# Who copies turned weights, z and values out of their banks: ScalarE by name instead of the tracer's choice, in an attention, feed-forward and state-space kernel

## The chip, the cores and the metric

The kernel runs on one core of one Trainium2 chip. The core has five engines, each with an instruction queue that it works off in order: TensorE (PE; its weight loads are listed apart as PEld), VectorE (DVE), ScalarE (ACT), GpSimd (POOL) and SyncE (SP, which here only issues DMAs). TensorE writes its results into eight banks of 128 x 512 fp32 each, the PSUM; they have to be copied or computed out of there by VectorE or ScalarE into the on-chip memory, the SBUF, before TensorE can take them as an operand again. The metric is device time in microseconds, the median of several executions.

## What is computed

Two sequences of 1024 rows of 256 numbers go through four residual layers, each on a layer norm of what came before:

```
x = x + attention(layernorm(x))            # 16 heads of 128, causal, ALiBi bias
x = x + ternary_ffn(layernorm(x))          # silu(gate) * up, rms norm, ternary weights
x = x + state_space(layernorm(x))          # in_proj, conv, scan over time, out_proj
x = x + kept_two_ffn(layernorm(x))         # silu(gate) * up, the 2 largest of 4 kept
```

The change lies in the attention, for which the reference is, cut:

```
q, k, v = x @ Wq.T, x @ Wk.T, x @ Wv.T                     # per head: (1024, 128)
scores = clip(q @ k.T / sqrt(128), -1024, 1024) + alibi_and_causal_mask
attn = softmax(scores)
out = sum over heads of (attn @ v) @ Wo_head.T
```

## The kernel before

The work is cut into four chunks k of 512 rows: sequence b = 0 or 1 and half u = 0 or 1 of it (`CH`). For each chunk the 16 heads of the attention are worked off one after another (`attention`, L397), and each head in four tiles j of 128 queries. A chunk with u = 1 sees 1024 keys; it takes the first 512 of k and v back from DRAM, where the chunk with u = 0 stored them head by head.

A step of a head is one tile j. In it:

- `scores` (L370): q times k into a bank `s` (PE, L377), clipped into the SBUF tile `ss` (VectorE, L381), the bias added and the row extreme `nm` found (VectorE, L387), then Exp with the row sum (ScalarE, L392).
- `turn` (L289), two steps later: PE turns the 128 x 128 blocks of the weights `ss` into a bank `pt` (L296), up to four blocks to a bank, and the bank is copied into `pT` (L299). A tile needs one such copy when u = 0 and two when u = 1: 2 x 16 x 4 x (1 + 2) = 384 in all, of 128 x 128, 256, 384 or 512 elements.
- `values` (L301), three steps later and only after each second tile, so for 256 queries at a time: v times the turned weights into a bank `z` (L308), copied into `zs`, 128 x 256 (L314): 128 copies.
- `project` (L316), four steps later: `zs` times the output weights into a bank `o` (L323); VectorE scales it and adds it to x (L329).
- for the next head, at tiles 0, 1 and 3: `queries`, `keys` (PE L336, copied with a scale by ScalarE, L343 and L350) and `new_values` (PE L360 into a bank `pv`, copied into `v`, 128 x 512, L365): 64 copies. If u = 0, SyncE then stores `v` in DRAM (L368).

The banks `pt`, `z`, `o`, `pq`, `pk` and `pv` are all taken in turn from one set of three (`ps_mm`, `ps_z`, L75), so each of these matmuls waits until the bank used three allocations before has been emptied. Two banks are for `s`, one for `y` of the state-space layer and two (`ps_r`) for the other layers.

While the heads of chunk k run, the remaining three layers of chunk k - 1 are worked off between them (`rest`, L969): after each step the loop at L992 draws as much of the other layers as its costs (`cost`, L974) make due. The last chunk's three layers come after all heads. The state-space layer is a scan over time on VectorE (L779, `hs`) for each of 64 pairs of a channel group and a state; ScalarE makes its decay `da` (L772) in a bank of `ps_r`, GpSimd its input `db` (L758) and its weighted output `hc` (L793), DMAs bring the rows `bs` and `cs` (L713), and PE sums the outputs up in `y` (L723). The softplus steps `se`, `sv`, `dl`, `sr` (L577 to L594) come once for each channel group.

The program is recorded by a tracer that lays out each engine's queue and sets the semaphores. An instruction written as `nc.scalar...` or `nc.vector...` goes to that engine; one written as `nc.any...` is given by the tracer to VectorE or ScalarE, one instruction at a time. The order in a queue is not strictly that of the program text. Besides the three copies of the change, `nc.any` stands at L148 (24 copies), L665 and L678 (4 each).

## Time and profile before

| | us |
|---|---|
| median of 3 runs | 1859.64 (1858.1 to 1860.81) |
| the profiled execution | 1863.3 |
| its span, first to last instruction | 1861.4 |
| PE busy | 1735.5 |
| DVE busy | 1308.0 |
| ACT busy | 947.3 |
| POOL busy | 821.3 |

How the three kinds of copies are shared out, with busy times:

| copy | on ScalarE | on VectorE |
|---|---|---|
| `pT` (L299) | 247, 115.8 us | 137, 69.7 us |
| `zs` (L314) | 56, 20.6 us | 72, 30.1 us |
| `v` (L365) | 53, 30.8 us | 11, 7.5 us |

Stages, in us from the span's start, read off from where each line runs: 0 to 280, chunk 0's heads alone, beside the preparation of ternary weights; 280 to 352, 790 to 838 and 1200 to 1268, heads beside the ternary feed-forward layer's end and the state-space layer's projections; 352 to 600, 838 to 1012 and 1268 to 1500, heads beside the scans of chunks 0, 1 and 2; 600 to 790, 1012 to 1200 and 1500 to 1640, heads beside the feed-forward layers; from 1640 on, chunk 3's other layers without heads.

A row of the profile names the line, the engine, the operation, what is written and read (out<-in, by the program's names without buffer numbers) and the shape. "Idle before" is the time that the engine stood still just before such instructions, with what ended it. PEclk and "granted clock" are the share of full speed that TensorE's clock was given.

### The profile page before, as it was taken

What the parts mean: (1) busy time and instruction counts of PE and PEld (TensorE: products, weight loads), DVE (VectorE), ACT (ScalarE), POOL (GpSimd) and SP (SyncE); (2) the same over time, 40 slices, a digit from 0 to 9 for tenths busy, and PEclk for the clock granted to TensorE, in tenths of its full rate; (3) what the DMA queues carried; (4) which work ended last, traced back from release to release, by engine and by line L of the source; (5) the groups of instructions that cost most, each with busy time, mean ns of one, the idle gap of its engine ahead of it and who ended that gap; (6) DMA issues with size and microseconds to landing.
All of it is one profiled execution on the core that took longest, in us unless ns stands there. A gap on an engine that the chain in (4) does not pass through costs nothing.

```text
span 1861.4 us, 25366 instructions
## 1 busy us (share of the span) xinstructions
PE 1735.5 (93%) x8468; PEld 1249.4 (67%) x8468; DVE 1308.0 (70%) x2552; ACT 947.3 (51%) x1736; POOL 821.3 (44%) x674
## 2 busy tenths in 40 slices
PE   8999999989989999997777999998998899998899
PEld 5777776566666667755555667765666676775895
DVE  5887656588875574568888465557888755857975
ACT  3445474545543553755554464565455436535742
POOL 3333040498873000418998001308898600035970
PEclk9999999989999999998989999999999899999999
DMA  6444412466652313127778424126675521212531
GB/s 192 153 145 156 151 57 86 145 213 206 201 182 83 105 51 121 56 93 234 217 230 233 142 68 141 39 85 225 196 229 172 168 100 50 74 53 77 183 129 62
DMA packets 178306, 256.07 MB, mean 138 GB/s; under 512 B 16240, under 2 KB 90992, under 8 KB 177152
## 3 DMA queue, kind: packets, MB, share of 16 engines
q1 hardware_dynamic: 176752, 241.61, 41.1%
q0 software_dynamic: 1152, 12.58, 1.8%
q8 instruction: 67, 1.10, 0.2%
q14 instruction: 63, 0.52, 0.1%
q10 hardware_dynamic: 272, 0.26, 0.0%
HBM read 232.04 MB, written 22.35 MB: 137 GB/s over the span
## 4 chain that ended last, share of the span: by engine, by line
PE 63%; DVE 11%; POOL 10%; issue 6%; DMA 5%; ACT 4%; SPq 1%; POOLq 0%; DVEq 0%; ACTq 0%
PE s L377 9%; PE z L308 8%; PE pq L336 5%; POOL hc L793 5%; PE pk L336 5%; PE pt L296 4%; PE o L323 4%; DVE hs L779 4%; PE pv L360 4%; POOL db L758 3%; PE g_g L463 3%; PE in L630 3%; PE u_g L463 3%; DMA cs<-bcd 3%; PE y L723 2%
## 5 line engine op out<-in xcount | busy, mean ns | idle before, releaser
L793 POOL TENSOR_TENSOR hc<-hs,cs 128x512 f32<-128x512 f32 x256 | 343.4, 1360 | 30.9 <-PE y L723 20.4
L381 DVE SCALAR_TENSOR_TENSOR ss<-s,lower 128x512 f32<-128x512 f32 (+3 forms) x384 | 205.5, 550 | 185.2 <-PE s L377 183.9
L392 ACT ACTIVATE ss<-ss,nm 128x128 f32<-128x128 f32 (+7 forms) x256 | 198.6, 776 | 255.1 <-DVE nm L387 238.3
L377 PE MATMUL s<-kT,qT 128*128 128x512 f32 (+3 forms) x768 | 301.6, 496 | 2.0 <-DVE ss L381 2.0
L758 POOL TENSOR_TENSOR db<-du,bs 128x512 f32<-128x512 f32 x192 | 267.1, 1400 | 67.2 <-DVE hs L779 44.8
L308 PE MATMUL z<-pT,v 128*128 128x256 f32 (+1 forms) x1280 | 274.0, 360 | 3.2 <-ACT pT L299 3.0
L308 PEld LDWEIGHTS z<-pT,v 128*128 128x128 f32 x1280 | 238.6, 191 | 49.3 <-ACT pT L299 4.9
L387 DVE CUSTOM_DVE_ANT_0 ss<-ss,alibi 128x128 f32<-128x128 f32 (+7 forms) x256 | 256.9, 1003 | 5.4
L772 ACT ACTIVATE da<-dl,a_neg 128x512 f32<-128x512 f32 x256 | 178.1, 697 | 140.5 <-DVE hs L779 110.7
L377 PEld LDWEIGHTS s<-kT,qT 128*128 128x128 f32 x768 | 134.9, 195 | 95.3 <-issue 85.1
L299 ACT COPY pT<-pt 128x512 f32<-128x512 f32 (+3 forms) x247 | 115.8, 486 | 161.7 <-PE pt L296 160.7
L779 DVE TENSOR_TENSOR_SCAN hs<-da,carry,db 128x512 f32<-128x512 f32 x128 | 160.0, 1270 | 31.2 <-POOL hc L793 19.8
L723 PE MATMUL y<-ident,hc 128*128 128x128 f32 x1024 | 152.5, 284 | 23.6 <-POOL hc L793 23.5
L296 PE MATMUL pt<-ident,ss 128*128 128x128 f32 x1152 | 170.9, 275 | 2.7 <-DVE x L329 2.7
L779 DVE TENSOR_TENSOR_SCAN hs<-da,db 128x512 f32<-128x512 f32 x128 | 153.2, 1210 | 19.0 <-POOL hc L793 11.0
L336 PE MATMUL pq<-xT_a,wq 128*128 128x512 f32 x256 | 135.8, 654 | 31.9 <-DVE zs L314 25.5
L723 PEld LDWEIGHTS y<-ident,hc 128*128 128x128 f32 x1024 | 125.1, 147 | 52.3 <-POOL hc L793 31.5
L296 PEld LDWEIGHTS pt<-ident,ss 128*128 128x128 f32 x1152 | 139.9, 142 | 18.1 <-DVE x L329 3.1
L323 PE MATMUL o<-wo,zs 128*128 128x256 f32 x512 | 135.6, 385 | 13.3 <-DVE zs L314 10.5
L360 PEld LDWEIGHTS pv<-wv,xT_a 128*128 128x128 f32 x1024 | 125.1, 197 | 18.1 <-ACT pT L299 14.1
L360 PE MATMUL pv<-wv,xT_a 128*128 128x128 f32 x1024 | 131.0, 282 | 5.0 <-ACT pT L299 4.6
L336 PE MATMUL pk<-xT_a,wk 128*128 128x512 f32 x256 | 127.1, 620 | 7.9 <-ACT qT L343 4.0
(204 smaller groups left out, 2547.7 us busy)
## 6 DMA issues: line engine op xcount, KB each, us to landing
cs<-bcd SPq DMA_DIRECT2D x256, 256.0 KB, 3.8
bs<-bcd SPq DMA_DIRECT2D x192, 256.0 KB, 4.5
alibi<-alibi_d SPq DMA_DIRECT2D x32, 512.0 KB, 4.7
wq<-in_wqT_dram SPq DMA_DIRECT2D x64, 128.0 KB, 2.6
wk<-in_wkT_dram SPq DMA_DIRECT2D x64, 128.0 KB, 2.5
wv<-in_wvT_dram SPq DMA_DIRECT2D x64, 128.0 KB, 3.2
wo<-in_woT_dram SPq DMA_DIRECT2D x64, 128.0 KB, 3.0
alibi<-alibi_d SPq DMA_DIRECT2D x32, 256.0 KB, 3.4
```

What stands on the lines that cost most here:

```text
L296: nc.tensor.transpose(tp[:, i, :], s[:, (kb0 + i) * P : (kb0 + i + 1) * P], ident)
L308: nc.tensor.matmul(zp[:, q0:W], lhsT=st["v_all"][:, kb, :], rhs=st["pts"][kb // 4][:, kb % 4, at * P + q0 : at * P + W], start=(kb == 0), ...
L323: ended["by"] = nc.tensor.matmul(op[:, i, :], lhsT=st["z"][half][:, i * P : (i + 1) * P], rhs=st["o"], start=True, stop=True,)
L336: nc.tensor.matmul(pp, lhsT=st[n][:, c, :], rhs=xT[:, c, :], start=(c == 0), stop=(c == KC - 1))
L360: nc.tensor.matmul(vp[:, t, :], lhsT=xT[:, c, t * P : (t + 1) * P], rhs=st["v"][:, c, :], start=(c == 0), stop=(c == KC - 1),)
L377: nc.tensor.matmul(sp[:, :n], lhsT=st["qT"][:, j * P : (j + 1) * P], rhs=st["kT"][:, k0 : k0 + n], start=True, stop=True,)
L381: nc.vector.scalar_tensor_tensor(s[:, k0 : k0 + n], sp[:, :n], CLIP, lower[:, S - W + k0 : S - W + k0 + n], op0=ALU.min, op1=ALU.max,)
L387: pace["tile"] = nc.vector.tensor_tensor_reduce(out=s[:, :W], in0=s[:, :W], in1=st["alibi"][:, :W], scale=1.0, scalar=3.0e38, op0=ALU.add, ...
L723: nc.tensor.matmul(yTs[c][:, t * P : (t + 1) * P], lhsT=h[:, t * P : (t + 1) * P], rhs=ident, is_transpose=True, start=start and t == 0, s ...
L758: nc.gpsimd.tensor_tensor(db[i], du, brow.pop(i), ALU.mult)
L779: nc.vector.tensor_tensor_scan(out=hs[i], data0=da.pop(i), data1=db.pop(i), initial=0.0 if first else carry[:, n, c : c + 1], op0=ALU.mult ...
L793: nc.gpsimd.tensor_tensor(hc[i], hs.pop(i), crow.pop(i), ALU.mult)
```

## The change

Three lines: the copy of the turned weights, the copy of z and the copy of the new values out of their banks are written as ScalarE's copy instead of the engine-neutral one. What is copied, where to, and the place in the program text stay.

```diff
@@ turn
-            nc.any.tensor_copy(st["pts"][kb0 // 4][:, 0:n, j * P : (j + 1) * P], tp[:, 0:n, :])
+            nc.scalar.copy(st["pts"][kb0 // 4][:, 0:n, j * P : (j + 1) * P], tp[:, 0:n, :])
@@ values
-        nc.any.tensor_copy(st["z"][half], zp[:, :W])
+        nc.scalar.copy(st["z"][half], zp[:, :W])
@@ new_values
-        nc.any.tensor_copy(v, vp)
+        nc.scalar.copy(v, vp)
```

## The prediction, made before the changed kernel was run

> **What bounds the kernel now.** I read the page's engine rows first, then the table of stages, then PE's waits in the stages where PE has gaps, then the chain of waits, the copies' own rows, and last one stall in order of time. From the page (engine: busy time, share of the span, instructions; then the granted TensorE clock in 40 slices):

> ```profile
> PE 1735.5 (93%) x8468; PEld 1249.4 (67%) x8468; DVE 1308.0 (70%) x2552; ACT 947.3 (51%) x1736; POOL 821.3 (44%) x674
> ...
> PEclk9999999989999999998989999999999899999999
> ```

> TensorE is the main bound, VectorE has more to do than ScalarE, and the clock dips in a few slices. The table of stages tells where (stage in us, its length, then busy time of PE, PEld, DVE, ACT, POOL with instruction counts, the granted clock, the DMA share, GB/s):

> ```profile
> 352.00:600.00 248.00, 223.86 (x1127) 164.87 (x1126) 197.19 (x353) 120.41 (x216) 188.31 (x137) 0.94 0.59 187
> 600.00:790.00 190.00, 188.74 (x858) 134.80 (x857) 107.78 (x244) 102.53 (x166) 24.26 (x21) 1.00 0.25 82
> ...
> 838.00:1012.00 174.00, 132.96 (x689) 95.18 (x687) 145.96 (x213) 88.55 (x182) 161.65 (x126) 0.94 0.76 228
> ...
> 1268.00:1500.00 232.00, 208.34 (x1037) 152.63 (x1036) 189.42 (x338) 113.84 (x204) 188.34 (x137) 0.94 0.61 193
> ```

> From 600 to 790 (attention beside a feed-forward layer) TensorE has 1.3 us of gaps; copies have nothing to win there, and the other stages without scans look the same (10.9 us of gaps from 0 to 280, mostly the first layer norm; 4 us or less in each of the rest). After 1640 there are no attention copies. So the change matters in the three stages with scans, C (352 to 600), E (838 to 1012) and G (1268 to 1500): PE gaps of 24, 41 and 24 us, and a clock of 0.94, worth 0.06 x 248 = 15, 10 and 14 us more. What ends PE's gaps in C (who waits <- for whom: us in total, times, longest):

> ```profile
> PE pq L336 <- DVE zs L314: 13.0, 5, 4.3
> PE o L323 <- DVE zs L314: 4.6, 2, 2.4
> PE pq L336 <- ACT zs L314: 2.5, 1, 2.5
> PE pv L360 <- ACT pT L299: 2.4, 2, 2.2
> ```

> Of 24 us, 17.6 wait for VectorE's copy of z (the weighted values) out of its bank; pq needs that bank, one of three, and o needs the copy itself. G answers alike: 12.5 + 2.9 = 15.4 of 23.5 us. In E, zs on VectorE ends only 3.0 of 41 us and hc on GpSimd 22.2; there the chain goes through the DMAs of cs, GpSimd's products and bs, so E hardly moves.

> How one such stall arises, in order of time (start, length, engine, line, operation, [idle before, and what ended it]):

> ```profile
> 381.90 1.89 DVE L387 CUSTOM_DVE_ANT_0 ss<-ss,alibi 128x640 f32<-128x640 f32 x1
> 382.04 0.68 ACT L772 ACTIVATE da<-dl,a_neg 128x512 f32<-128x512 f32 x1
> ...
> 383.73 1.74 DVE L591 TENSOR_TENSOR sr<-se,sr 128x512 f32<-128x512 f32 x1
> 383.84 0.83 ACT L392 ACTIVATE ss<-ss,nm 128x640 f32<-128x640 f32 x1 [1.12 <-DVE nm L387]
> ...
> 385.39 2.32 DVE L779 TENSOR_TENSOR_SCAN hs<-da,db 128x512 f32<-128x512 f32 x2
> ...
> 387.68 0.41 DVE L314 COPY zs<-z 128x256 f32<-128x256 f32 x1
> ...
> 388.15 1.22 PE L336 MATMUL pq<-xT_a,wq 128*128 128x512 f32 x1 [4.33 <-DVE zs L314]
> ```

> The last z matmul ends at 381.7. Its copy takes 0.41 us but stands 5.9 us in VectorE's queue, behind a score reduction, a softplus step and two scans. ScalarE is idle meanwhile, from 382.7 to 383.8 and again for 1.87 us before 386.6, each time held by an instruction that itself waits for VectorE.

> **The change part by part.** Of 576 copies (384 pT, 128 zs, 64 v), 356 are ScalarE's already (247 + 56 + 53); for these only the writing changes. 220 change engine:

> ```profile
> L299 ACT COPY pT<-pt 128x512 f32<-128x512 f32 x142 | 81.2, 580 | 128.4 <-PE pt L296 127.5
> ...
> L299 DVE COPY pT<-pt 128x512 f32<-128x512 f32 x50 | 34.1, 681 | 2.2 <-PE pt L296 2.1
> L314 DVE COPY zs<-z 128x256 f32<-128x256 f32 x72 | 30.1, 418 | 24.9 <-PE z L308 24.7
> ```

> (count | busy us, mean ns | idle before.) VectorE loses 50 x 0.681 + 42 x 0.547 + 34 x 0.279 + 11 x 0.412 for pT, 72 x 0.418 for zs and 11 x 0.682 for v: 34.1 + 23.0 + 9.5 + 4.5 + 30.1 + 7.5 = 108.7 us, and goes from 1308 to about 1200. ScalarE gains the same shapes at its own rows (580, 473, 252, 373; 368; 580 ns): 29.0 + 19.9 + 8.6 + 4.1 + 26.5 + 6.4 = 94.5 us, from 947 to 1042, 56% of the span. Both totals lie beside TensorE's 1735 and are no time by themselves.

> Out of banks, then, ScalarE is 15% shorter on the same shape (580 against 681 ns). [...]

> In C the moves are 24 pT, 13 zs and 2 v (12.7 + 5.4 + 1.4 = 19.4 us off VectorE), in G 23, 11 and 2 (17.6 us), in E 6, 8 and 1 (6.1 us). C's ScalarE rises by some 17 us, from 120 to 137 of 248.

> *PE's stalls.* In C and G together the 24 zs on VectorE cost PE 17.6 + 15.4 = 33.0 us, the 8 on ScalarE 5.0 us: 0.63 each. The 81 pT on ScalarE (42 + 39) cost 2.9 + 4.4 = 7.3 us, 0.09 each; the 47 on VectorE nothing. If copies that move fare like those already there: zs 32 x 0.63 = 20 instead of 38, pT 47 x 0.09 = 4.2 more, net 13.8 us fewer stalls.

> *The clock.* After the 4.33 us stall the clock reads 0.50 from 388.1 to 391.9 and four pq take 3.78 us; after one of 2.44 us before 371.3 it reads 0.50 from 373 to 375; after one of 1.40, from 416 to 418, it reads 1.00. Over C and G 28.8 us of clock loss stand beside 47.4 us of gaps, 0.61 for each, so 13.8 us of stalls bring 8.4 more: 22 us of PE time at best. [...]

> *Not all of it reaches the end.* Cut to C and G, the chain of waits spends 157 us on PE, 138 on VectorE, 86 on GpSimd. VectorE's moved copies hold 8.0 us of it directly (zs 3.1 + 2.4, pT 1.2 + 1.4); ScalarE, with 9% of its time on the chain (22 of 234), gives back 0.09 x 32 = 3. So the least gain by this reading is 5 us, the most 22. I take 14, near the middle: PE and VectorE hold similar shares of this chain.

> *What waits behind a moved copy.* On ScalarE: da (which feeds the scans), Exp, qT and kT. Copies of 0.25 to 0.58 us are covered there: da's own idle time before it, held by scans that have not freed its bank, is 110.7 us in the whole run, and no scan waits for da among VectorE's larger waits. If that cover went, the most is the 32 us added in C and G. v's DMA on SyncE follows its copy; the stored values are read a whole chunk later, so this costs nothing, at worst 11 x 0.58 = 6 us if each were waited for.

> *Order.* The tracer lays out each queue anew, and neighbours may move as well. No row prices that; I bound it by the stalls at stake, 22 us either way, and take nothing.

> **The sum.** The profiled execution took 1863.3 us (span 1861.4), 3.7 above the median of 1859.6. 1863.3 - 14 = 1849.3, and on the median's footing 1845.6: **1846**.

> **The rivals.**
> - *Slower: the copies queue behind a waiting Exp.* ScalarE works strictly in order, and its longest wait is Exp for VectorE's nm: 238.3 us in all, 50.9 in C, 47.8 in G. Before 415.8 it stood 3.79 us so, just when VectorE's zs ended a PE stall of 1.40. A zs placed after such an Exp comes 0.99 + 0.19 us later (Exp's mean in C, and its read of the sum), although z was ready. The deciding point: 32 r + 4.2 = 38.0, so beyond r = 1.06 us of stall for each zs the stages get longer (the eight seen have 0.63). If all 24 moved ones pay 1.18 more, PE loses 28 + 4 us before the clock's share; if half do, 14 + 4. With some of it off the chain: +4 to +30, most likely 1874. For it: at 415.8 VectorE took zs just while ScalarE stood held. Against: ScalarE is half idle and freeing VectorE also brings nm earlier.
> - *Much faster.* All zs stalls of C and G go: 38 + 0.61 x 38 = 61 us of PE time, of which VectorE (178 of C's 248 left) and GpSimd (188) let half through: 30 to 45, so 1815 to 1830.
> - *No change in time.* The copies move, the stages stay held by GpSimd's products and the DMAs of bs and cs, as E is now: 1856 to 1863. Should the written engine do less than it says (the 356 already there), it ends here too.

> **How the numbers follow.** Forecast (gain 5 to 22, so 1838 to 1855) 0.47; much faster 0.10; no change 0.13; slower 0.30. About 0.2% (3.7 us) is what a measurement of this kernel can tell from no change. Faster 0.57, same 0.13, slower 0.30. The range reaches into both outer cases, 1822 to 1877, and leaves out some 0.06 below and 0.12 above.

> **What would show it.** Right: all 576 copies as ACT; DVE near 1200 and ACT near 1042; PE's waits for zs in C and G down from 38 to about 20; clock there 0.95 or more; C and G each about 7 us shorter; all else in place. Wrong: "PE <- ACT zs" or "PE <- ACT pT" of 30 us or more, with ScalarE held by nm just before; or stalls gone and C and G as long, ended by hc, db or bs.

## The result: 1880.0 us, slower by 1.15%

The changed kernel takes 1880.01 us (median of 4 runs, 1878.54 to 1885.05) where the kernel before takes 1859.66: a ratio of 1.0115 with a 95% interval of 1.0095 to 1.0135. The forecast was 1846 in a range of 1822 to 1877; the time lies above both. For the copies of z the mechanism is that of the rival "the copies queue behind a waiting Exp", which had 0.30 and a price of 1874; the sign that the prediction named for it came, PE waiting 56.4 us for zs on ScalarE. More than half of the loss, though, comes only when the turned weights are forced to ScalarE too, and how it does was not isolated.

The profiled execution took 1880.1 us, its span is 1878.3, 16.9 more than before. From its page (engine: busy us, share, instructions; then the granted clock):

```profile
PE 1735.7 (92%) x8468; PEld 1248.4 (66%) x8468; DVE 1218.1 (65%) x2331; ACT 1018.0 (54%) x1957; POOL 820.3 (44%) x674
...
PEclk9999999999999999998998999999999999999999
```

PE's work is the same to 0.2 us. The copies moved as announced: 221 instructions fewer on VectorE and 221 more on ScalarE, VectorE relieved by 90 us. Yet the span grew. Where, tells the table of stages of the kernel after, cut at the same points of the work (stage, length, busy PE, PEld, DVE, ACT, POOL with counts, clock, DMA share, GB/s): first chunk 0's heads, then C, E and G.

```profile
20.30:224.00 203.70, 202.76 (x1031) 145.68 (x1030) 144.52 (x395) 106.71 (x285) 58.28 (x51) 1.00 0.47 154
356.00:609.00 253.00, 223.23 (x1126) 163.89 (x1125) 182.80 (x314) 133.37 (x255) 188.80 (x137) 0.95 0.58 184
848.00:1026.50 178.50, 135.77 (x692) 99.17 (x690) 142.29 (x199) 92.63 (x198) 161.92 (x126) 0.92 0.71 222
1282.00:1517.30 235.30, 204.64 (x1040) 150.45 (x1039) 178.49 (x302) 125.68 (x239) 188.81 (x137) 0.96 0.59 190
```

Chunk 0's heads, which the prediction counted as untouched, in the kernel before:

```profile
20.60:220.60 200.00, 199.84 (x1031) 146.56 (x1030) 158.81 (x425) 98.29 (x253) 57.18 (x51) 1.00 0.48 156
```

So chunk 0 lost 3.7 us, C 5.0, E 4.5 and G 3.3: 16.5 of the 16.9. VectorE has 14 us less to do in C and ScalarE 13 more, and the stage became longer. PE's waits in C, now (who <- for whom: us, times, longest):

```profile
PE pq L336 <- ACT zs L314: 17.5, 6, 5.6
PE o L323 <- ACT zs L314: 8.1, 4, 2.9
PE pv L360 <- ACT pT L299: 1.8, 1, 1.8
```

25.6 us for zs, where it was 20.1 (17.6 on VectorE, 2.5 on ScalarE); in G it is 26.2 instead of 17.9. The stall that the prediction showed at 388 is still there, at the same point of the work, in the kernel after (start, length, engine, line, operation, [idle before, and what ended it]):

```profile
385.94 1.88 DVE L387 CUSTOM_DVE_ANT_0 ss<-ss,alibi 128x640 f32<-128x640 f32 x1
...
387.86 0.83 ACT L392 ACTIVATE ss<-ss,nm 128x640 f32<-128x640 f32 x1 [1.10 <-DVE nm L387]
388.60 0.19 ACT L392 ACTIVATION_READ_ACCUMULATOR ss<-ss,nm 128x1 f32 x1
388.69 0.35 ACT L314 COPY zs<-z 128x256 f32<-128x256 f32 x1
...
389.09 3.53 PE L336 MATMUL pq<-xT_a,wq 128*128 128x512 f32 x4 [4.60 <-ACT zs L314]
```

The copy left VectorE's queue, in which it stood behind a softplus step and two scans, and now stands on ScalarE behind an Exp that waits for VectorE. The stall was 4.33 us and is 4.60. Where nothing else is in the way one sees the loss bare, in chunk 0. One head before:

```profile
87.16 1.02 PE L377 MATMUL s<-kT,qT 128*128 128x512 f32 x2
87.18 0.08 DVE L387 DVE_READ_ACCUMULATOR2_ANT nm<- 128x1 f32 x1
87.25 0.42 DVE L314 COPY zs<-z 128x256 f32<-128x256 f32 x1
87.36 0.61 ACT L392 ACTIVATE ss<-ss,nm 128x384 f32<-128x384 f32 x1 [1.47 <-DVE nm L387]
...
88.02 1.03 PE L323 MATMUL o<-wo,zs 128*128 128x256 f32 x4
```

and the same head after:

```profile
88.21 1.02 PE L377 MATMUL s<-kT,qT 128*128 128x512 f32 x2
88.24 0.61 ACT L392 ACTIVATE ss<-ss,nm 128x384 f32<-128x384 f32 x1 [1.31 <-DVE nm L387]
88.76 0.19 ACT L392 ACTIVATION_READ_ACCUMULATOR ss<-ss,nm 128x1 f32 x1
88.86 0.35 ACT L314 COPY zs<-z 128x256 f32<-128x256 f32 x1
...
89.26 1.13 PE L323 MATMUL o<-wo,zs 128*128 128x256 f32 x4
```

When nm is done, VectorE is free for the copy and ScalarE starts the Exp. Before, the two ran side by side, and o began 0.86 us after s. After, the copy follows the Exp, and o begins 1.05 us after s. That is 0.19 us at most heads. The chunk's 3.7 us are 0.23 for each of its 16 heads. A head's other copy of z has slack: there o begins 2.31 us after the end of z in both kernels.

### The profile page after: what moved, and what is told of

It reads as the page before. It is cut to its first block, busy times and chain, and to the rows that moved or that the text cites. A ratio compares the mean times of both kernels' runs of the same rounds, so it can differ in the third digit from the quotient of the medians.

```text
span 1878.3 us, 25340 instructions
## 1 busy us (share of the span) xinstructions
PE 1735.7 (92%) x8468; PEld 1248.4 (66%) x8468; DVE 1218.1 (65%) x2331; ACT 1018.0 (54%) x1957; POOL 820.3 (44%) x674
## 4 chain that ended last, share of the span: by engine, by line
PE 60%; POOL 12%; DVE 10%; issue 7%; DMA 5%; ACT 5%; SPq 1%; POOLq 0%; DVEq 0%; ACTq 0%
PE s L377 8%; PE z L308 7%; POOL hc L793 6%; PE pq L336 5%; PE pk L336 5%; POOL db L758 4%; PE pt L296 4%; PE o L323 4%; PE pv L360 4%; DVE hs L779 3%; PE g_g L463 3%; PE in L630 3%; PE u_g L463 3%; DMA bs<-bcd 3%; PE y L723 2%
## 5 line engine op out<-in xcount | busy, mean ns | idle before, releaser
L793 POOL TENSOR_TENSOR hc<-hs,cs 128x512 f32<-128x512 f32 x256 | 339.3, 1343 | 33.6 <-PE y L723 27.3
L392 ACT ACTIVATE ss<-ss,nm 128x128 f32<-128x128 f32 (+7 forms) x256 | 198.6, 776 | 243.6 <-DVE nm L387 227.9
L308 PE MATMUL z<-pT,v 128*128 128x256 f32 (+1 forms) x1280 | 272.9, 360 | 5.3 <-ACT pT L299 4.5
L308 PEld LDWEIGHTS z<-pT,v 128*128 128x128 f32 x1280 | 238.4, 191 | 50.5 <-ACT pT L299 7.0
L387 DVE CUSTOM_DVE_ANT_0 ss<-ss,alibi 128x128 f32<-128x128 f32 (+7 forms) x256 | 258.2, 1009 | 5.6 <-DVE ss L381 0.2
L772 ACT ACTIVATE da<-dl,a_neg 128x512 f32<-128x512 f32 x256 | 178.1, 699 | 138.3 <-DVE hs L779 112.8
L299 ACT COPY pT<-pt 128x512 f32<-128x512 f32 (+3 forms) x384 | 172.0, 476 | 147.7 <-PE pt L296 146.2
L779 DVE TENSOR_TENSOR_SCAN hs<-da,carry,db 128x512 f32<-128x512 f32 x128 | 159.6, 1269 | 38.4 <-POOL hc L793 24.5
L779 DVE TENSOR_TENSOR_SCAN hs<-da,db 128x512 f32<-128x512 f32 x128 | 154.4, 1216 | 36.2 <-POOL db L758 18.1
L296 PE MATMUL pt<-ident,ss 128*128 128x128 f32 x1152 | 172.6, 277 | 0.6 <-ACT pT L299 0.6
L336 PE MATMUL pq<-xT_a,wq 128*128 128x512 f32 x256 | 134.4, 651 | 37.5 <-ACT zs L314 35.8
L323 PE MATMUL o<-wo,zs 128*128 128x256 f32 x512 | 139.5, 393 | 20.9 <-ACT zs L314 20.6
L296 PEld LDWEIGHTS pt<-ident,ss 128*128 128x128 f32 x1152 | 140.7, 143 | 17.1 <-ACT pT L299 3.3
L323 PEld LDWEIGHTS o<-wo,zs 128*128 128x128 f32 x512 | 96.4, 195 | 69.3 <-ACT zs L314 42.1
L360 PEld LDWEIGHTS pv<-wv,xT_a 128*128 128x128 f32 x1024 | 123.2, 195 | 16.4 <-ACT pT L299 12.7
L360 PE MATMUL pv<-wv,xT_a 128*128 128x128 f32 x1024 | 128.7, 279 | 3.8 <-ACT pT L299 3.7
```

Of the source, the lines that this page charges most:

```text
L296: nc.tensor.transpose(tp[:, i, :], s[:, (kb0 + i) * P : (kb0 + i + 1) * P], ident)
L308: nc.tensor.matmul(zp[:, q0:W], lhsT=st["v_all"][:, kb, :], rhs=st["pts"][kb // 4][:, kb % 4, at * P + q0 : at * P + W], start=(kb == 0), ...
L323: ended["by"] = nc.tensor.matmul(op[:, i, :], lhsT=st["z"][half][:, i * P : (i + 1) * P], rhs=st["o"], start=True, stop=True,)
L336: nc.tensor.matmul(pp, lhsT=st[n][:, c, :], rhs=xT[:, c, :], start=(c == 0), stop=(c == KC - 1))
L360: nc.tensor.matmul(vp[:, t, :], lhsT=xT[:, c, t * P : (t + 1) * P], rhs=st["v"][:, c, :], start=(c == 0), stop=(c == KC - 1),)
L387: pace["tile"] = nc.vector.tensor_tensor_reduce(out=s[:, :W], in0=s[:, :W], in1=st["alibi"][:, :W], scale=1.0, scalar=3.0e38, op0=ALU.add, ...
```

## The experiments

**Theory A:** what a copy of z costs is what stands ahead of it in its engine's queue. On ScalarE that is Exp, which runs about 1 us (0.99 on average in C of the kernel before) or waits for nm (238.3 us in all there), and in the scan stages the decay da, which waits for a scan (110.7 us). **Rivals:** B, the load of the other 148 moved copies delays ScalarE's own work; C, writing an engine by name lays all queues out anew, and that costs; D, formed after the first four runs, turned weights forced to ScalarE cost something of their own. Ratios are to the kernel before, run on the same chip; it took 1858.5 to 1858.9 us on the three chips of these runs and 1859.7 beside the changed kernel, so a difference of about 1 us between versions run on different chips means nothing. Added lines shift line numbers beyond 380 by one to three in some of these kernels.

**z alone.**

```diff
-        nc.any.tensor_copy(st["z"][half], zp[:, :W])
+        nc.scalar.copy(st["z"][half], zp[:, :W])
```

> Only the 128 copies of z are written as ScalarE's; turned weights and values stay with the tracer. Theory A (a copy of z on ScalarE stands behind an Exp that runs or waits for VectorE's nm, and PE waits for the copy): most of the 20 us come back, 1872 to 1882, with PE waiting over 50 us for zs on ScalarE. Rival B (the other 148 moved copies load ScalarE and delay Exp and the decays): 1856 to 1864. Rival C (any such edit lays the queues out anew, and that costs): anything between 1862 and 1885, with PE's waits for zs near the 44 us of before.

1866.0 us, 1.0036 (1.0021 to 1.0051): slower, but by a third of what the whole change costs. Chunk 0's heads take 203.8 us as in the changed kernel, so that part belongs to z alone. PE waits 47.4 us for zs. The tracer had given VectorE 159 turned weights instead of 137. A had too much and B too little; only C's wide range holds the time.

**Turned weights and values alone.**

```diff
-            nc.any.tensor_copy(st["pts"]...)
+            nc.scalar.copy(st["pts"]...)
-        nc.any.tensor_copy(v, vp)
+        nc.scalar.copy(v, vp)
```

> Only turned weights and values are written as ScalarE's; z stays with the tracer. Theory A: the time of before or a little less, 1852 to 1863, since z can still go to VectorE where ScalarE is held. Rival B: 1873 to 1882, since 68 of the 94.5 us of load are in it. Rival C: 1862 to 1885.

1861.8 us, 1.0024 (1.0011 to 1.0037). Load alone is not the cause: 68 of the 94.5 us of moved ScalarE time are in this kernel, and it costs 3 us. B falls as the whole cause. But 7.5 + 3.3 is only half of the 20.4 us that the whole change costs; the lines cost more together than apart.

**z on VectorE, the others on ScalarE.**

```diff
-        nc.scalar.copy(st["z"][half], zp[:, :W])
+        nc.vector.tensor_copy(st["z"][half], zp[:, :W])
```

> Turned weights and values are ScalarE's by name, all copies of z VectorE's by name. Theory A: 1850 to 1862; the per-head time of chunk 0 is back at 12.65 us or below, from 12.95, and what remains of PE's waits for zs is in the scan stages, behind scans, some 30 to 45 us in all. Rival B: 1873 or more. Rival C: 1865 to 1885 with no wait that explains it.

1871.6 us, 1.0068 (1.0049 to 1.0087). A's forecast fails in size. Chunk 0 is back at 199.8 us, as A says, though ten of its copies stand 1.0 us behind the score reduction (L387) on VectorE: they are the copies with slack, and o still begins 2.31 us after z. But in the scan stages z waits on VectorE as it waited on ScalarE:

```profile
PE pq L336 <- DVE zs L314: 28.2, 10, 4.8
PE y L723 <- POOL hc L793: 26.0, 18, 4.6
PE o L323 <- DVE carry L788: 11.9, 4, 3.6
PE o L323 <- DVE zs L314: 9.0, 7, 1.9
```

The four waits put down to `carry` are for zs too: o reads zs, and at each of the four (the first at 369.8 us) it starts 0.05 us after the end of a copy of z that stood behind two scans; the next carry copy happens to end at the same moment. So PE waits 37.2 + 11.9 = 49.1 us for zs, against 43.7 in the kernel before and 56.4 in the changed one. Neither engine is good by itself.

**The changed kernel with one order altered: Exp behind the copy of z of its step.** Engine and load are those of the change.

```diff
+        ended["zs"] = nc.scalar.copy(st["z"][half], zp[:, :W])
...
                 for f in now:
                     f()
+                with tc.issue_after(ended["zs"].ins) if ended["zs"] else nullcontext():
+                    exp()
```

> All three copies stay ScalarE's as in the changed kernel; only the order on ScalarE differs: the Exp of a step is put behind the copy of z of that step. The engine and the load are those of the change, so rival B gives 1878 to 1882. Theory A gives 1852 to 1866: chunk 0's head back at 12.65 us, PE's waits for zs down from 56 to under 30 us; the price is an Exp that comes later, which the two steps until its weights are turned should cover. Rival C: no direction.

The Exp is recorded after the step's other work in every step, and tied behind the copy of z where the step has one. 1853.5 us, 0.9971 (0.9952 to 0.9990): from 20 us slower to 5 us faster by order alone. Chunk 0's heads take 199.5 us. PE waits 33.8 us for zs, a little over the 30 expected; pq's part falls from 35.8 us to 8.2:

```profile
PE o L323 <- ACT zs L314: 25.6, 11, 4.2
...
PE pq L336 <- ACT zs L314: 8.2, 7, 1.9
```

This shows A for Exp. What z still waits for in this kernel's trace is almost all da. In the changed kernel the copies of z start 156 us after the end of their z, summed over the 128, 84 of them behind Exp and 48 behind da; here, of 96 us between the end of z and its copy's start, 81 are decays that run or wait for scans.

**The engines of before, written by name.** The engine of each of the 576 copies is taken from a list.

```diff
+    chosen = lambda kind: nc.vector.tensor_copy if next(by[kind]) == "1" else nc.scalar.copy
-        nc.any.tensor_copy(st["z"][half], zp[:, :W])
+        chosen("z")(st["z"][half], zp[:, :W])
```

> Every one of the 576 copies is written with the engine that it had in the kernel before (356 ScalarE, 220 VectorE, by a list), so that no copy changes engine and only the writing does; some copies come to stand earlier among ScalarE's decays in the scan stages. Theory A (it is the engine, by what a copy of z then stands behind): within 0.3% of before, 1853 to 1864. Rival C (writing the engine lays the queues out anew, and that costs): 1868 or more.

1856.8 us, 0.9990 (0.9981 to 0.9999). No copy changed engine, and the time stayed. C falls: it is not the writing.

**z alone by name, Exp behind it.**

> Only z is ScalarE's by name, and the Exp of its step stands behind it; turned weights and values stay with the tracer. The Exp-behind-z version with all three on ScalarE gave 1853.5. Theory A, that the order of z and Exp is all: 1848 to 1858, no worse than that. Theory D (with turned weights forced to ScalarE too, its queue has no outlet, which is why all three cost 21 us and z alone 7.5): clearly below it, 1840 to 1850.

The edit is that of z alone with the order of Exp-behind-z. 1844.6 us, 0.9925 (0.9909 to 0.9942), 9 us below the version with all three by name. D holds beside A: forcing turned weights and values costs, whatever the order of z.

**Exp also behind the copies of turned weights.**

```diff
-            nc.scalar.copy(st["pts"]...)
+            ended["zs"] = nc.scalar.copy(st["pts"]...)
```

> As the Exp-behind-z version, with the Exp also behind that step's copies of the turned weights. Theory A says that z is what PE waits for, and turned weights have a step of slack: no gain, 1850 to 1862, or a small loss, because Exp comes later. If the copies of turned weights behind an Exp cost too (theory D), 1842 to 1850.

1857.1 us, 0.9990 (0.9979 to 1.0000), 3.6 above Exp behind z only, the medians' difference. Putting Exp behind the turned weights gains nothing on balance, as A said. This speaks against Exp ahead of them as D's cost; that a gain there and a loss from the later Exp cancel is not excluded.

**Exp and the decays behind the copy of z.**

```diff
+                with tc.issue_after(ended["copy"].ins) if paced else nullcontext():
                     nc.scalar.activation(da[i], parts[c][0], AF.Exp, scale=a_neg[:, c, n : n + 1])
```

> As the Exp-behind-z version, with the decays of the scan stages also put behind the latest copy of z. In that version 81 of the 96 us that z's copies still wait are decays that run or wait for the scans. If PE's remaining 34 us of waits for zs are what holds the scan stages: 10 to 20 us less, 1834 to 1845, PE's waits for zs under 15 us. If the decays have no slack: the scans start later, VectorE waits for da, and the time rises to 1858 to 1885.

1831.6 us, 0.9854 (0.9840 to 0.9869), a little below the range expected. All three copies are on ScalarE, as in the change, and the time is 48 us below it. PE's waits in that kernel:

```profile
PE y L725 <- POOL hc L796: 27.6, 21, 4.6
PE pk L336 <- ACT pT L299: 11.6, 10, 2.3
PE yb L814 <- ACT ysb L811: 10.3, 7, 2.1
...
PE o L323 <- ACT zs L314: 3.8, 2, 3.3
```

and, first in the list of all its waits:

```profile
ACT zs L314 <- PE z L308: 247.3, 103, 8.9
```

ScalarE now stands idle 247 us before copies of z (46 in the changed kernel), with decays and Exps queued behind them, and the kernel is faster for it: PE's waits for zs go from 56.4 us in the changed kernel to 3.8. The order also holds back the scans (VectorE's waits for da before them are 56.3 us, 4.1 in the changed kernel), so VectorE may come to nm sooner (ScalarE's waits for nm fall from 227.9 us to 130.9); what that adds was not separated.

**Only the decays behind z, Exp where it was.**

> The changed kernel with only the decays put behind the latest copy of z, Exp where it was. With both behind z the time was 1831.6, with Exp alone 1853.5, with none 1880. Theory A (an Exp ahead of z costs by itself, and so does a decay): the decays' share comes back, the Exp's stays, 1852 to 1866, with chunk 0's head still at 12.95 us, since there are no decays there. If only the decays mattered in the scan stages: 1832 to 1842.

The edit of the decays alone, on the changed kernel. 1848.2 us, 0.9936 (0.9917 to 0.9954), between the two ranges. Chunk 0's heads take 203.7 us, just as in the changed kernel, against 199.5 with both: where there are no decays, the Exp's share stays whole. Of the 48 us that both orders bring, the decays alone bring 32 and Exp alone 26.5; each costs by itself.

**z on VectorE, with the scans behind it.** On top of the version with z on VectorE:

```diff
                 with (
                     tc.issue_after(pace["front"].ins) if paced else nullcontext(),
+                    tc.issue_after(ended["copy"].ins) if paced else nullcontext(),
                 ):
                     nc.vector.tensor_tensor_scan(
```

> As the version with z on VectorE by name and the other two on ScalarE (1871.6), with each scan put behind the latest copy of z on VectorE. If the place in the queue decides and not the engine: 1845 to 1862, PE's waits for zs on VectorE down from 37 us to under 20. If scans cannot be put back without loss (VectorE is the busier engine there): 1868 to 1890.

1829.5 us, 0.9844 (0.9827 to 0.9860), 42 us below the same kernel without that line, and beyond what was expected. PE's waits for zs were 49.1 us there, with the four listed under `carry`. They are 12.7 now, and none is listed under `carry`:

```profile
PE pv L360 <- ACT pT L299: 14.8, 10, 2.0
PE pq L336 <- DVE zs L314: 12.3, 6, 3.3
```

With the order set right, z on VectorE (1829.5) and z on ScalarE (1831.6) are alike. The place decides, not the engine.

**z and values by name.**

> The change without its line on turned weights: z and values by name. z alone was 1866, all three 1880. If the turned weights forced to ScalarE are what comes on top (theory D): 1863 to 1869. If the 11 copies of values do it: 1875 or more.

The change without its line on turned weights: 1868.5 us, 1.0057 (1.0042 to 1.0072). So the turned weights hold 11.5 of the change's 20 us on top of z, as D expected, and the values, against z alone, 2.5, no more than the intervals' width.

**z alone by name, Exp and decays behind it.**

> z by name with Exp and decays behind it, turned weights and values left to the tracer. From 1831.6 (all three by name, both behind) and the 9 us that leaving the turned weights free saved beside Exp-behind-z: 1820 to 1830 if the two add up, 1830 to 1836 if the order has already removed what an outlet to VectorE would save.

1821.3 us, 0.9798 (0.9783 to 0.9812): the best version, 2.0% faster than the kernel before and 3.1% faster than the changed one. The two effects add up. Set out by what is named (rows) and what is put behind z (columns), medians in us:

| | nothing | Exp | decays | both |
|---|---|---|---|---|
| z, turned weights, values | 1880.0 | 1853.5 | 1848.2 | 1831.6 |
| z alone | 1866.0 | 1844.6 | not run | 1821.3 |
| difference | 14.0 | 8.9 | | 10.3 |

The last line is what forcing turned weights and values to ScalarE costs, in each of the three orders that were run for both. How it comes about was not isolated. PE's waits for copies of turned weights, on either engine, do not tell: when those are left free, the waits fall from 24.9 us to 15.2 with both orders, but rise from 13.7 to 28.8 with Exp alone behind z and from 10.5 to 18.4 with nothing behind it, and the time falls in all three. A run that moves turned weights only where PE waits for them was not made.

## Why the prediction was wrong, point by point

- **The failed step: "If copies that move fare like those already there".** 0.63 us of stall for each z was taken from the 8 copies that ScalarE had in C and G. Measured after the change, over all 32: (17.5 + 8.1 + 18.3 + 7.9) / 32 = 1.62; the rival's deciding point was 1.06. Followed copy by copy through both traces, the 8 cost 3.8 us, 0.5 each, after 5.0, while the 24 that moved cost 48.0 us, 2.0 each, where on VectorE they had cost 33.0, 1.4 each. The 8 were no sample of the 24: they are four places, seen once in C and once in G, and their 5.0 us are two stalls, both behind a decay. They had not been free of ScalarE's queue either: six of them stood 1.7 to 2.8 us behind an Exp or a decay, and PE stalled for only two. The rate for those moved would have had to be read from what ScalarE's queue held when each z ended, and the rows at 383.8 and 415.8 showed that an Exp held it.
- **"ScalarE is idle meanwhile"** was true and no help. In the kernel after, ScalarE stands idle 1.10 us before the Exp at 387.86 because that waits for nm, and is not free for the copy behind it, which starts 5.4 us after the end of its z. The stall at 388 went from 4.33 to 4.60 us; with the same engine it is 1.9 us when Exp stands behind z, and gone when the decays do too.
- **"Copies have nothing to win there"**, of stages without gaps on PE: true, but there was something to lose. Chunk 0 lost 3.7 us, with PE's gaps only 0.8 us larger by the rows; the other 2.9 us are counted as busy, 202.76 us after 199.84 for the same 1031 matmuls.
- **E "hardly moves"**: it lost 4.5 us. PE's wait for hc there grew from 22.2 to 29.1 us, while its waits for zs fell from 5.7 to 3.9. Cut at the same score matmuls, E takes 173.6 us before, 177.5 in the changed kernel, 173.1 with z alone and 175.5 with turned weights and values alone: z alone loses nothing there, the other two kinds lose 1.9. By what way, no run separates.
- **The rate for turned weights, 0.09 us each**: in C and G the waits are 6.0 us for 128, 0.05 each. Right as a wait, and yet turned weights cost 11.5 us on top of z. The prediction had 4.2 us for them and no other term.
- **The clock**, 0.61 us for each us of gaps: gaps for zs grew by 14 us in C and G, and the clock rose, 0.95 and 0.96 after 0.94. The wrong rate made no difference to the sign.
- **The loads**: VectorE 1218 for "about 1200", ScalarE 1018 for 1042. Neighbouring instructions overlap in the rows (88.76 + 0.19 ends after 88.86), so sums of durations overstate busy time: the three kinds of copies did bring ScalarE 94.8 us of durations, for 94.5 forecast, but its busy time grew by 70.7.
- **"Order ... take nothing"** held for what was meant: with the engines of before written by name, the tracer's new layout changed the time by 1.7 us. But the place of a moved copy in its new queue is a matter of order too, and had no term outside the rival: order alone is worth 48 us here, with the engines of the change kept, where the bound was 22.
- **The slower rival** had the mechanism, and its price 14 was low against 20: it had no chunk 0 (3.7) and no E (4.5). It counted 4 us for turned weights, where 11.5 came with them.

## What to carry to other kernels

A copy that frees a bank or feeds TensorE should stand in its queue ahead of work that waits for another engine and has slack itself; ask for each such copy what is ahead of it when its input is ready, not how busy its engine is. Moving such a copy to a half-idle engine can lose what another place in the same queue would win: here engine alone +1.15%, order on the same engine -1.46%, and with the other copies left free -2.0%. A rate taken from the few cases that a scheduler chose need not hold for the cases that it refused: here 0.5 us for the one kind and 2.0 for the other.
